# Order and queues of the first loads in a fused LoRA and gated feed-forward kernel

## The chip, the cores and the metric

The kernel runs on one core of one Trainium2 chip. The metric is the device time of one execution, in microseconds. The kernel before took 476.14 us (median of three runs, 475.85 to 476.36).

## The reference

The input x has 8 sequences of 256 tokens with 1024 features. Each sequence picks one of 8 adapters of rank 16; the adapted tokens pass a gated feed-forward layer whose operands are rounded to 8-bit floats, and x is added again:

```python
B_sel = B[adapter_ids]; A_sel = A[adapter_ids]
Bx  = einsum('bni,bri->bnr', x, B_sel)
h   = einsum('bnr,bor->bno', Bx, A_sel)
gate = fake_quant_fp8(h) @ gate_w.T * gate_w_scale      # 2752 x 1024
up   = fake_quant_fp8(h) @ up_w.T * up_w_scale          # 2752 x 1024
hidden = silu(gate) * up
out  = x + fake_quant_fp8(hidden) @ down_w.T * down_w_scale   # 1024 x 2752
```

The weights come as float32 values that are already rounded to 8 bits.

## The kernel before

The 2048 tokens are cut into four blocks of 512 (t = 0 to 3), the features into eight rows of 128 (k), the inner dimension into 22 chunks (c; the last one is half as wide). Activations lie transposed, features on partitions and tokens along the free dimension. Block t of x is `xs[t]`, 128 x 8 x 512 float32, 2 MB.

For each block TensorE first computes `bx` = B x (`two_times_b`, 64 small matmuls for blocks 0 and 1, each of which contracts 128 features of 128 tokens with one adapter's B). Two copies bring the result into SBUF as `bm`, and `two_times_a` multiplies it by A (64 small matmuls into `c`), which VectorE and ScalarE scale and round to 8 bits as `xg[t]`. Then `gate_up(c, t)` computes sixteen matmuls of 128 x 512 into two accumulators `y`, eight for the gate and eight for the up half. ScalarE applies the SiLU and VectorE the product, which is `hid[c]`. One weight tile `w_gu` of 1 MB holds both halves of a chunk; five buffers hold them. The first five chunks run for block 0, then for block 1, then for blocks 2 and 3 together; the other chunks run for all four blocks each. At last the down projection (`yd`) runs over eight output rows, and VectorE adds x. ScalarE also sums the low bits of the weights and the squares of the activations beside all this, as guards for a general path that is not taken here.

TensorE's instructions are kept in program order. The opening of that order is: sixteen matmuls on zeros (`warm`), `bx` of block 0 with four more filler matmuls after row k = 3, seven fillers, the `c` matmuls, `gate_up(0, 0)` in the order "two rows of gate, two of up", then the next chunks:

```python
pass_time(warm, 16, TB)
bm = two_times_b(0, lambda k: pass_time(warm, 4) if k == 3 else None)
pass_time(warm, 7)
two_times_a(0, bm)
gate_up(0, 0, turns=(2, 2, 2, 2))
```

Row k of `bx` needs the B of both sequences of the block and row k of x; `c` needs all of A for the block. The first half of tile w0 serves the first eight y matmuls of `gate_up(0, 0)`, its second half the last eight; `gate_up(1, 0)` needs w1.

The loads are issued on the queues of the engines. `adapter_of` (line 363) loads an adapter's number into a register of the issuing engine, which must wait for the transfer of `ids`; `load_b` (line 366) and `load_a_two` (line 373) use it as an address. `load_x` is line 381, `load_gate_up` line 391. Almost everything goes through SyncE's queue, in program order; ScalarE issues `ids` and one B. DMA issues share eight completion semaphores in turn, so an issue can wait for the landing of the one eight places ahead. The array `x4` holds x in pieces of `PIECES[t]` rows each, each piece contiguous; block 0 is cut 4, 3, 1.

A DMA of the down projection's tail weights (`wt`, line 656) stands late in the program but is issued after block 3's loads, ahead of weight tile 5.

Of the kernel before, what the change touches and what calls it, by code (L numbers as in the profile page):

```python
# [25 lines left out]
NH = H // P  # L26
# [9 lines left out]

KS = NH // 2

PIECES = ((4, 3, 1), (4, 3, 1), (NH,), (NH,))
FP8_MAX = 448.0  # L40

SAME_MAX = 240.0
# [17 lines left out]
def x_of(x4, t, k):  # L60

    first = 0
    for n in PIECES[t]:
        if k < first + n:
            break
        first += n
    at = (t * NH + first) * P * TB
    piece = x4[at : at + n * P * TB].rearrange("(p k n) -> p k n", p=P, k=n)
    return piece, first
# [214 lines left out]
def adaln_ffn(  # L284
# [13 lines left out]
    nc = tc.nc  # L298
# [31 lines left out]
    wt = kept.tile([P, NH, P], F32, name="w_dt")  # L330
# [6 lines left out]
    with ExitStack() as fast:  # L337
# [5 lines left out]
        xs = [acts.tile([P, NH, TB], F32, name=f"x{t}") for t in range(NTB)]  # L343
# [8 lines left out]
        b_two = [lora.tile([P, 2 * BROW + R], F32, name=f"b{t}") for t in range(2)]  # L352
# [9 lines left out]
        def adapter_of(batch, queue):  # L362
            return queue.value_load(ids_i[0:1, batch : batch + 1], min_val=0, max_val=7)  # L363

        def load_b(b, i, adapter, queue):
            queue.dma_start(  # L366
                out=b[:, i * BROW : (i + 1) * BROW], in_=b8[bass.ds(adapter * P, P), :]
            )

        def load_a_two(t, j, adapter):  # L370
            for g in range(2):
                row = 32 * (2 * g + j) + R * j
                nc.sync.dma_start(
                    out=a_two[t][row : row + R],
                    in_=a8[bass.ds(adapter * 2 * R + g * R, R), :],
                )

        def load_x(t, k):
            piece, first = x_of(x4, t, k)
            ks = slice(first, first + piece.shape[1])  # L380
            nc.sync.dma_start(out=xs[t][:, ks, :], in_=piece)

        w_of = {}

        def load_gate_up(c, parts=1):
            n = NH if c == NI - 1 else 2 * NH
            w = wpool.tile([P, 2 * NH, P], F32, tag="w", name="w_gu")[:, :n]
            src = gate_up_of(w_gu, c).rearrange("p (k n) -> p k n", n=P)
            n //= parts
            for i in range(parts):  # L390
                nc.sync.dma_start(out=w[:, bass.ts(i, n)], in_=src[:, bass.ts(i, n)])
            w_of[c] = w

        load_x(0, 0)
        load_b(b_two[0], 0, adapter_of(0, nc.scalar), nc.scalar)
        second = adapter_of(1, nc.sync)
        load_b(b_two[0], 1, second, nc.sync)


        load_x(0, 4)  # L400
        load_a_two(0, 1, second)
        load_a_two(0, 0, adapter_of(0, nc.sync))
        load_x(0, 7)
        for c in range(NFIRST):
            load_gate_up(c, parts=1 if c else 2)
        adapters = [adapter_of(2 + q, nc.sync) for q in range(6)]
# [4 lines left out]
        for j in range(2):  # L411
            load_a_two(1, j, adapters.pop(0))

        for t in (2, 3):
            load_x(t, 0)
            for q in (2 * t - 4, 2 * t - 3):
                load_b(b_four, q, adapters[q], nc.sync)
        for q in range(4):
            nc.sync.dma_start(
                out=a_four[32 * q : 32 * q + R], in_=aT[bass.ds(adapters[q] * R, R), :]  # L420
# [48 lines left out]
        def multiply(*args, **kwargs):  # L469
            tc.keep_in_program_order(nc.tensor.matmul(*args, **kwargs))  # L470

        def pass_time(to, n, size=P):

            for i in range(n):
                multiply(
                    to[:, :size],
                    lhsT=zeros[:, :P],
                    rhs=zeros[:, :size],
                    start=(i == 0),
                    stop=(i == n - 1),  # L480
                )

        def times_b(bx, b, n, quads, between=None):


            for k in range(NH):
                for q, (i, row, t, cols) in enumerate(quads):
                    at = i * BROW + k * R - row
                    multiply(
                        bx[q][32 * q : 32 * (q + 1)],  # L490
                        lhsT=b[:, at : at + 32],
                        rhs=xs[t][:, k, cols],
                        start=(k == 0),
                        stop=(k == NH - 1),
                    )
                if between:
                    between(k)

        def two_times_b(t, between=None):


            n = SEQ // 2
            quads = [
                (j, R * j, t, slice(at, at + n))
                for half in range(2)
                for j in range(2)
                for at in (j * SEQ + half * n,)
            ]
            bx = [psum.tile([P, n], F32, tag="ps", name=f"bx{half}") for half in range(2)]
            times_b([bx[q // 2] for q in range(4)], b_two[t], n, quads, between)  # L510
            bm = lora.tile([P, 2, n], F32, tag="bm2", name="bm2", bufs=2)
            for other in range(2):
                for half, copy in enumerate((nc.vector.tensor_copy, nc.scalar.copy)):
                    to = half ^ other
                    tc.keep_in_program_order(
                        copy(  # L516
                            bm[64 * to : 64 * (to + 1), other],
                            bx[half][64 * half : 64 * (half + 1)],
                        )
                    )  # L520
            return bm
# [110 lines left out]

        warm = psum.tile([P, TB], F32, tag="ps", name="warm")
        pass_time(warm, 16, TB)
        bm = two_times_b(0, lambda k: pass_time(warm, 4) if k == 3 else None)
        pass_time(warm, 7)
        two_times_a(0, bm)
        gate_up(0, 0, turns=(2, 2, 2, 2))
# [14 lines left out]
        for c in range(NFIRST, NI):  # L653
            load_gate_up(c)
            if c == NI - 2:
                nc.sync.dma_start(out=wt, in_=w_d_tail)
            for t in range(NTB):
                gate_up(c, t)

# [70 lines left out]
        for k in range(NH - 1):  # L730
# [23 lines left out]
            first = k % 2 == 0  # L754
# [29 lines left out]
    with found_others.Else():  # L784

        k = NH - 1
# [9 lines left out]
        t, cols = NTB - 1, slice(cut, TB)  # L796
# [88 lines left out]
```

## Time and profile before

| | us |
|---|---|
| median of three runs | 476.14 |
| the profiled execution, whole time | 477.12 |
| its span, first to last instruction | 475.3 |
| TensorE busy | 469.8 |
| ScalarE busy | 192.5 |
| VectorE busy | 105.6 |
| GpSimd busy | 1.0 |

The page gives the busy time of each engine and the share of the span. The chain follows the work that ended last backwards, at each step to what released it. A timeline lists instructions in order of time, equal neighbours merged, with the idle time before them and what ended it in brackets; "SPq" is SyncE's queue issuing a DMA, and its length is that of the issue, not of the transfer. Of 53.44 MB that the DMA engines moved, most belong to later stages; over the first 17.21 us they moved 320 GB/s on average, afterwards 105 GB/s. The granted TensorE clock is full throughout.

Landings of the first transfers (issue plus time to landing): x rows 0 to 3 at 5.8 us, B at 6.1 and 6.2, x rows 4 to 6 at 8.3, x row 7 at 9.6, w0's first half at 10.9, w1 at 17.2.

### The profile page before, as it was taken

How to read it: one execution, taken by the hardware profiler on the slowest of the kernel's cores; microseconds unless marked ns; L12 is line 12 of the kernel's file. 1: busy time of each engine (PE TensorE's matmuls, PEld its weight loads, DVE VectorE, ACT ScalarE, POOL GpSimd, SP SyncE). 2: the span in 40 equal slices, each digit the busy share in tenths (PEclk: the TensorE clock that was granted, in tenths of full speed). 3: DMA queues.
4: the chain of work that ended last, by engine and by line, in shares of the span. 5: the costliest groups of instructions: out<-in, count | busy, mean ns of one | idle time of the engine just before them, and what ended most of it. 6: DMA issues, size and time to landing. Idle time of an engine off the chain costs nothing.

```text
span 475.3 us, 6009 instructions
## 1 busy us (share of the span) xinstructions
PE 469.8 (99%) x2514; PEld 217.0 (46%) x2514; DVE 105.6 (22%) x163; ACT 192.5 (40%) x249; POOL 1.0 (0%) x7
## 2 busy tenths in 40 slices
PE   8999999999999999999999999999999999999997
PEld 4454544444444444444444444444444444444444
DVE  1333432121212222121212212132120121031031
ACT  1322447995556654533454554359212022021000
POOL 0000000000000000000000000000000000000000
PEclk9999999999999999999999999999999999999999
DMA  8995013422222112222211111123335255063031
GB/s 291 406 405 186 1 48 133 176 88 90 88 88 89 24 66 89 90 88 88 90 30 60 44 62 56 61 83 123 103 146 161 64 185 161 22 213 114 3 116 66
DMA packets 13780, 53.44 MB, mean 112 GB/s; under 512 B 1650, under 2 KB 2930, under 8 KB 10674
## 3 DMA queue, kind: packets, MB, share of 16 engines
q1 hardware_dynamic: 13600, 52.92, 32.1%
q8 instruction: 21, 0.34, 0.3%
q14 instruction: 13, 0.11, 0.1%
q10 hardware_dynamic: 146, 0.07, 0.0%
HBM read 44.60 MB, written 8.39 MB: 111 GB/s over the span
## 4 chain that ended last, share of the span: by engine, by line
PE 96%; DMA 3%; SPq 0%; issue 0%; DVE 0%
PE y L470 62%; PE yd L470 31%; DMA w_gu<-w_gu 2%; PE c L470 1%; PE bx L470 1%; DMA x<-x 1%; DMA ids_i<-ids 0%; SPq L363 0%; SPq L366 0%; DVE o L695 0%; PE count L470 0%
## 5 line engine op out<-in xcount | busy, mean ns | idle before, releaser
L470 PE MATMUL y<-xg,w_gu 128*128 128x512 fp8e4 x1376 | 298.4, 379 | 0.9 <-DMA w_gu<-w_gu 0.9
L470 PEld LDWEIGHTS <-w_gu 128*128 128x128 bf16 x1376 | 134.0, 98 | 163.8 <-DMA w_gu<-w_gu 1.8
L470 PE MATMUL yd<-hid,w_d 128*128 128x512 fp8e4 (+2 forms) x693 | 146.0, 373 | 0.0
L609 ACT ACTIVATE g<-y,gate_s 128x512 f32<-128x512 f32 (+1 forms) x88 | 59.8, 681 | 137.2 <-PE y L470 137.2
L610 DVE SCALAR_TENSOR_TENSOR hid<-y,up_by_down,g 128x512 fp8e4<-128x512 f32 x84 | 63.1, 751 | 220.3 <-PE y L470 162.2
L470 PEld LDWEIGHTS <-w_d 128*128 128x128 bf16 x693 | 66.6, 98 | 79.0 <-issue 1.7
L456 ACT ACTIVATE junk<-w_d 128x1408 bf16<-128x1408 uint16 (+1 forms) x16 | 21.2, 1324 | 88.4 <-DMA w_d<-w_d 88.3
L695 DVE SCALAR_TENSOR_TENSOR o<-yd,down_s,x 128x512 f32<-128x512 f32 x28 | 20.0, 748 | 107.4 <-PE yd L470 92.8
L456 ACT ACTIVATE junk<-w_gu 128x2048 bf16<-128x2048 uint16 (+1 forms) x22 | 41.0, 1863 | 0.0
L463 ACT ACTIVATE junk<-hid 128x2048 bf16<-128x2048 fp8e4 x21 | 40.0, 1905 | 0.4
L463 ACT ACTIVATE junk<-xg 128x2048 bf16<-128x2048 fp8e4 x8 | 15.3, 1909 | 0.3
L528 ACT ACTIVATE xg<-c,inv 128x512 fp8e4<-128x512 f32 x16 | 9.7, 688 | 8.6 <-PE c L470 8.6
L526 DVE TENSOR_SCALAR xg<-c,inv 128x512 fp8e4<-128x512 f32 x16 | 10.9, 744 | 2.8 <-PE c L470 2.8
L470 PE MATMUL warm<-zeros 128*128 128x512 bf16 (+1 forms) x27 | 6.5, 402 | 1.2 <-DVE zeros L309 1.2
L695 DVE SCALAR_TENSOR_TENSOR o<-yd,down_s,xg 128x512 f32<-128x512 f32 (+2 forms) x5 | 3.2, 644 | 12.3 <-PE yd L470 12.3
L516 ACT COPY bm<-bx 64x128 f32<-64x128 f32 x4 | 1.0, 262 | 9.7 <-PE bx L470 9.6
L470 PE MATMUL bx<-x,b 128*32 128x128 f32 x128 | 4.3, 276 | 0.6 <-DMA x<-x 0.6
L470 PEld LDWEIGHTS <-zeros 128*128 128x128 bf16 x27 | 2.6, 116 | 4.7 <-issue 3.0
L470 PE MATMUL c<-bm,a 32*128 32x128 f32 x128 | 4.3, 277 | 0.0
L456 ACT ACTIVATION_READ_ACCUMULATOR junk<-w_gu 128x1 f32 x22 | 4.2, 191 | 0.0
L470 PEld LDWEIGHTS c<-bm,a 32*128 32x128 f32 x128 | 3.9, 186 | 0.5 <-ACT bm L516 0.4
L470 PE MATMUL yd<-hid_tail,w_dt 64*128 64x512 bf16 (+1 forms) x32 | 4.1, 377 | 0.0
(47 smaller groups left out, 41.0 us busy)
## 6 DMA issues: line engine op xcount, KB each, us to landing
w_gu<-w_gu SPq DMA_DIRECT2D x20, 1024.0 KB, 4.8
outT<-o SPq DMA_DIRECT2D x31, 256.0 KB, 2.2
w_d<-w_d SPq DMA_DIRECT2D x8, 704.0 KB, 4.8
w_d<-w_d SPq DMA_DIRECT2D x8, 640.0 KB, 3.9
x<-x SPq DMA_DIRECT2D x2, 2048.0 KB, 11.1
x<-x SPq DMA_DIRECT2D x2, 1024.0 KB, 8.6
x<-x SPq DMA_DIRECT2D x2, 768.0 KB, 9.5
w_gu<-w_gu SPq DMA_DIRECT2D x3, 512.0 KB, 3.8
```

The source lines that it names most:

```text
L456: nc.scalar.activation(junk_like(w), low(w), AF.Copy, accum_out=lows[:rows, column : column + 1])
L463: nc.scalar.activation(junk_like(q), q, AF.Square, accum_out=squares[:rows, column : column + 1])
L470: tc.keep_in_program_order(nc.tensor.matmul(*args, **kwargs))
L516: copy(bm[64 * to : 64 * (to + 1), other], bx[half][64 * half : 64 * (half + 1)],)
L526: nc.vector.tensor_scalar(to, c, scale, None, ALU.mult, saturate=False)
L528: nc.scalar.activation(to, c, AF.Copy, scale=scale, saturate=False)
L609: nc.scalar.activation(g[rows], gates, AF.Silu, scale=gate_s[: gates.shape[0]])
L610: nc.vector.scalar_tensor_tensor(to, in0=ups, scalar=up_by_down[rows], in1=g[rows], op0=ALU.mult, op1=ALU.mult, saturate=False,)
L695: nc.vector.scalar_tensor_tensor(o, in0=y, scalar=down_s, in1=x, op0=ALU.mult, op1=ALU.add)
```

## The change

Block 0 of x is cut into pieces of 2, 2, 3 and 1 rows. They are the first four issues on SyncE's queue, and the first five weight tiles follow at once. Both loads of B for block 0 go on ScalarE's queue, the four loads of A on GpSimd's, each with its own register load. The four filler matmuls move from behind row 3 to behind row 6. Later on, x of blocks 2 and 3 and the tail weights are each loaded in two halves instead of one transfer. The amount of data and all other arithmetic stay.

```diff
-PIECES = ((4, 3, 1), (4, 3, 1), (NH,), (NH,))
+PIECES = ((2, 2, 3, 1), (4, 3, 1), (NH,), (NH,))
...
-        def load_a_two(t, j, adapter):
+        def load_a_two(t, j, adapter, queue=nc.sync):
             for g in range(2):
                 row = 32 * (2 * g + j) + R * j
-                nc.sync.dma_start(
+                queue.dma_start(
...
-        def load_x(t, k):
+        def load_x(t, k, n=NH):
             piece, first = x_of(x4, t, k)
-            ks = slice(first, first + piece.shape[1])
-            nc.sync.dma_start(out=xs[t][:, ks, :], in_=piece)
+            n = min(n, piece.shape[1])
+            nc.sync.dma_start(out=xs[t][:, k : k + n, :], in_=piece[:, k - first : k - first + n])
...
-        load_x(0, 0)
-        load_b(b_two[0], 0, adapter_of(0, nc.scalar), nc.scalar)
-        second = adapter_of(1, nc.sync)
-        load_b(b_two[0], 1, second, nc.sync)
-
-
-        load_x(0, 4)
-        load_a_two(0, 1, second)
-        load_a_two(0, 0, adapter_of(0, nc.sync))
-        load_x(0, 7)
+
+
+        for k in (0, 2, 4, 7):
+            load_x(0, k)
+        for j in range(2):
+            load_b(b_two[0], j, adapter_of(j, nc.scalar), nc.scalar)
+            load_a_two(0, j, adapter_of(j, nc.gpsimd), nc.gpsimd)
         for c in range(NFIRST):
             load_gate_up(c, parts=1 if c else 2)
...
         for t in (2, 3):
-            load_x(t, 0)
+            for k in (0, KS):
+                load_x(t, k, KS)
...
-        bm = two_times_b(0, lambda k: pass_time(warm, 4) if k == 3 else None)
+        bm = two_times_b(0, lambda k: pass_time(warm, 4) if k == 6 else None)
...
-                nc.sync.dma_start(out=wt, in_=w_d_tail)
+                for ks in (slice(0, KS), slice(KS, NH)):
+                    nc.sync.dma_start(out=wt[:, ks], in_=w_d_tail[:, ks])
```

## Prediction

> **What bounds the kernel now.** I read the page's busy table, then the chain that ended last, then TensorE's and SyncE's instructions over the first microseconds.
>
> ```profile
> span 475.3 us, 6009 instructions
> PE 469.8 (99%) x2514; PEld 217.0 (46%) x2514; DVE 105.6 (22%) x163; ACT 192.5 (40%) x249; POOL 1.0 (0%) x7
> ```
>
> TensorE is idle for 475.3 - 469.8 = 5.5 us. Of this, 2.8 us is the tail after 472.50 and 1.2 us precedes the first warm-up matmul; what waits for data is all in the opening. The chain in order of time says where it hands over to TensorE for good:
>
> ```profile
> 3.33 4.97 DMA x<-x
> ...
> 8.32 8.85 DMA w_gu<-w_gu
> 17.17 0.05 issue
> 17.21 13.12 PE y L470 x60
> ```
>
> The last two columns ahead of the name are start and length. From 17.21 us on everything is TensorE, back to back. What sets that point is the landing of the second weight tile, w1. TensorE's timeline:
>
> ```profile
> 1.20 5.58 PE L470 MATMUL warm<-zeros 128*128 128x512 bf16 x16 [1.20 <-DVE zeros L309]
> 6.71 1.08 PE L470 MATMUL bx<-x,b 128*32 128x128 f32 x32
> ...
> 8.34 0.86 PE L470 MATMUL bx<-x,b 128*32 128x128 f32 x24 [0.22 <-DMA x<-x]
> 9.59 0.43 PE L470 MATMUL bx<-x,b 128*32 128x128 f32 x8 [0.38 <-DMA x<-x]
> ...
> 10.45 2.17 PE L470 MATMUL c<-bm,a 32*128 32x128 f32 x64
> 12.58 1.89 PE L470 MATMUL y<-xg,w_gu 128*128 128x512 fp8e4 x8
> 14.70 1.90 PE L470 MATMUL y<-xg,w_gu 128*128 128x512 fp8e4 x8 [0.23 <-DMA w_gu<-w_gu]
> 17.21 2.98 PE L470 MATMUL y<-xg,w_gu 128*128 128x512 fp8e4 x13 [0.62 <-DMA w_gu<-w_gu]
> ```
>
> Two waits for x, two for weights. At the steady pace (13.12 us / 60 = 219 ns) sixteen y matmuls need 3.5 us; here 17.21 - 12.58 = 4.63 us, so the weights cost 1.13 us. SyncE's queue shows why data are late:
>
> ```profile
> 0.75 0.38 SPq L381 DMA_DIRECT2D x<-x  x1
> 2.92 0.37 SPq L366 DMA_DIRECT2D b<-b  x1
> 3.33 0.45 SPq L381 DMA_DIRECT2D x<-x  x1
> 4.00 2.58 SPq L373 DMA_DIRECT2D a<-a  x4
> 6.62 0.42 SPq L381 DMA_DIRECT2D x<-x  x1
> 7.09 2.99 SPq L391 DMA_DIRECT2D w_gu<-w_gu  x6
> ```
>
> B, A and the register loads stand between the x pieces, so the weights are not asked for before 7.09 us. The one-microsecond windows show what that costs: 418, 404, 406 and 412 GB/s from 3 to 7 us, then
>
> ```profile
> 7.00:8.00 1.00, 1.00 (x36) 0.75 (x24) 0.00 (x0) 0.00 (x0) 0.00 (x0) 1.00 0.92 275
> 8.00:9.00 1.00, 0.78 (x27) 0.59 (x24) 0.00 (x0) 0.00 (x0) 0.00 (x0) 1.00 0.85 293
> ```
>
> The last column is GB/s.
>
> **What the Trainium skill says.** "DMA: Bandwidth & Descriptors", section "SWDGE vs HWDGE vs iDMA": a DMA from GpSimd gets its descriptors from software on that engine, one from SyncE or ScalarE from hardware. The kernel before issues none from GpSimd, so no trace shows its price here. The same page, "Issuing engines are not separate DMA queues": all issuers share the same 16 engines, and more issuers save only issue time. That fits: the stream runs near 410 GB/s from one queue. "TensorE: Matmul & The Clock Gate", Part 1: a cold TensorE runs at half rate, and about 3.4 us of idling makes it cold. In the trace the warm-up's weight loads are 0.43 us apart until about 5.3 us, then twice as dense; no later gap reaches 1 us.
>
> **The change part by part.**
>
> *SyncE's queue.* Removed from it ahead of the weights: one B, four A and two register loads. Ahead of them stay four x pieces at about 0.42 us each, so the issues start at 0.75, 1.17, 1.6 and 2.05 us and the first half of w0 at 2.5 us instead of 7.09. Behind it w0's second half waits for the landing of ids (1.93 us now), and w1 to w4 wait for the four x pieces, because completion semaphores are reused; more than 1 MB is outstanding at each such point, so the DMA engines don't run dry.
>
> *x.* The pieces hold 2.10 MB, with B (0.14) and A (0.13) 2.37 MB. By 3.0 us 0.21 MB had moved (66 and 147 GB/s in two windows). At 410 GB/s the rest takes 5.3 us, 8.3 us in all; before, a piece landed some 0.8 us after its bytes were through by this sum (the second piece: 7.45 against 8.30). So the last x lands near 9.1 us, instead of 9.57 (6.62 plus 2.9 to landing). I allow 8.8 to 9.5.
>
> *B.* ScalarE issues its first at 2.88 us as now. The second comes after another register load and address step (0.27 + 0.15 + about 0.3 us) at about 4.05 us and lands 3.2 us later (what the first took): 7.25 us instead of 6.2. Now the bx matmuls start at 6.71, when warm-up ends; this moves them to 7.25. Without waits the 64 take 1.9 us (as 30.34 to 32.22 us for the next block), the four filler matmuls 0.25: 9.4 us. The last x at 9.1 is hidden behind them, so the bound is about even. bx ends near 9.5 instead of 9.9, and c can start near 10.1 instead of 10.45.
>
> *A on GpSimd.* Its memset ends at 1.55 us; the ids land at 1.93, the register is ready near 2.85. Lower end: issues as short as SyncE's 0.33 us and a landing in 4.1 us (today's median): 2.85 + 4 x 0.33 + 0.55 for the second register + 4.1 = 8.8 us. Upper end: the price on "DMA: Bandwidth & Descriptors", "Anatomy of one DMA — SWDGE (gpsimd) path", is 2.0 us fixed plus bytes at 436 GB/s, 2.08 us for 32 KB; four of them end to end give 2.85 + 8.3 + 0.55 = 11.7 us, more if the loaded engines delay them. I take 1 us of GpSimd each, as an estimate between these: the last is issued at 6.4 us and lands at 8.5 to 10.5. Nothing else queues on GpSimd but a branch at the end; behind A stand only the c matmuls. A is thus just hidden behind bx.
>
> *Where the stall goes.* c at 10.1 gives y at 12.23 (2.13 later, as 10.45 to 12.58) and the second y group at 15.75, if w1 is there. So w1 remains the last to arrive. Its start is set by bytes: now it lands at 17.17, and the windows from 7 to 17 us fall short of 410 GB/s by 0.52 MB, or 1.25 us. The change fills the holes that come from late issue but not those of small rows: B's 544 byte rows, the 2 KB rows of A and of the last x piece are still there. I take two thirds, 0.84 us: w1 at 16.35 us. The bounds are 0.3 and 1.3 us (zero if all holes are small rows; more than 1.3 would need a faster first 3 us).
>
> *Later edits.* Halving x of blocks 2 and 3 and the down tail adds three issues of about 0.4 us on SyncE, before a wait for a weight buffer that lasts 30.3 us (42.5 to 67.5): hidden. Block 1's x is issued after w0 has landed and moves with the stream: its last piece lands at 30.5 now (17.2 + 13.3) and is needed near 31.8. With both 0.8 us earlier the slack stays 1.3 us. If that cover failed, the cost would be microsecond for microsecond.
>
> *Sum.* 17.21 to 16.37 us: -0.84 us. All 455 us behind shift as they are: profiled span 475.3 to 474.5, this execution's 477.12 to 476.3. The median of the runs is 0.98 lower than that execution; the difference carries over: 476.14 - 0.84 = 475.3.
>
> **The rivals.** *Fully packed stream.* If w1 lands by 15.75 to 16.2, the gain is 1.0 to 1.45 us: 474.7 to 475.1. For it: two thirds of the holes stand exactly where issues were late. Against it: the engines show 0.85 to 0.92 busy inside them, so they were not empty.
>
> *A late on GpSimd (the slower side).* It decides from the point where the last A lands after 17.21 - 3.5 - 2.13 = 11.6 us. At 2.6 us each the last lands at 2.85 + 10.4 + 0.55 = 13.8: +2.2 us, 478.3; at 3 us each 15.4: +3.8 us, 479.9. For it: four dependent-looking small transfers on one software path into a full stream; ready time is 1 us short of what the upper price gives. Against it: 5 us of room if issues overlap.
>
> *B's second half late.* It decides at 17.21 - 3.5 - 2.13 - 0.7 - 2.15 = 8.7 us, against 7.25; at 10 us it would be +1.3 us, 477.4.
>
> *Hidden anyway.* If w1 comes as late as now because all SDMA bytes before it are the same, the time stays 475.9 to 476.1.
>
> **How the numbers follow.** A measurement of this kernel can tell about 0.2%, 0.95 us, from no change. Main case with "hidden anyway", 475.2 to 476.4: 0.40. Packed stream, 474.7 to 475.2: 0.28. A late, 477.1 to 480: 0.25. B late, 477.1 to 478: 0.07. So faster 0.28, same 0.40, slower 0.32. The range leaves out about 0.1 above and 0.07 below: 474.8 to 478.6; the likeliest case's own is 475.2 to 476.4.
>
> **What the profile after would show.** Right: weight issues from 2.5 us, no x wait over 0.2 us, c near 10.1 us, a y start after w1 near 16.4, DMA above 380 GB/s from 3 to 12 us. Wrong: c waiting for DMA a beyond 11.6 us, bx waiting for b beyond 8.7, or GpSimd issues well over 1 us each. A gap of more than 3.4 us would also cost clock: sixteen matmuls at half rate, 3.5 us more.

## The result, and the profile after

The changed kernel took 481.96 us (median of four runs, 480.86 to 482.47), the kernel before 476.25 (four runs, one more than above): a ratio of 1.0114, interval 1.0090 to 1.0138. The change costs 5.7 us, where a gain of 0.8 us was forecast.

The page of the changed kernel:

```profile
span 480.0 us, 6020 instructions
PE 470.7 (98%) x2514; PEld 218.3 (45%) x2514; DVE 105.5 (22%) x163; ACT 192.6 (40%) x249; POOL 3.1 (1%) x11
```

The span of the profiled execution grew by 4.7 us, TensorE's busy time by 0.9 us. Idle time is 9.3 us instead of 5.5. The chain that ended last in order of time (start, length, what) names the new hand-over:

```profile
4.17 7.65 DMA b<-b
11.82 0.04 issue
11.86 3.14 PE bx L468 x54
...
16.18 2.11 PE c L468 x63
18.29 16.52 PE y L468 x76
```

Before, the chain ran through x and the weights. Now it runs through the second B: 7.65 us from issue at 4.17 to landing at 11.82. TensorE's timeline of the changed kernel:

```profile
1.33 5.21 PE L468 MATMUL warm<-zeros 128*128 128x512 bf16 x16 [1.33 <-DVE zeros L309]
9.97 0.38 PE L468 MATMUL bx<-x,b 128*32 128x128 f32 x2 [3.43 <-DMA b<-b]
11.86 3.14 PE L468 MATMUL bx<-x,b 128*32 128x128 f32 x54 [1.51 <-DMA b<-b]
...
16.11 2.18 PE L468 MATMUL c<-bm,a 32*128 32x128 f32 x64
18.25 5.12 PE L468 MATMUL y<-xg,w_gu 128*128 128x512 fp8e4 x23
```

The waits for x and for weights are gone; y runs without a break from 18.25. In their place stand two waits for B. The first two bx matmuls use the first sequence's B and start at 9.97; the next need the other B and start at 11.86, instead of 6.71.

The one-microsecond windows show a second effect; the third number from the end is the granted clock of TensorE, the last is GB/s:

```profile
5.00:6.00 1.00, 1.00 (x7) 0.45 (x5) 0.00 (x0) 0.00 (x0) 0.48 (x1) 1.00 0.82 281
...
11.00:12.00 1.00, 0.14 (x4) 0.14 (x8) 0.00 (x0) 0.00 (x0) 0.00 (x0) 0.70 1.09 388
12.00:13.00 1.00, 1.00 (x24) 0.92 (x25) 0.00 (x0) 0.00 (x0) 0.00 (x0) 0.50 1.03 422
...
14.00:15.00 1.00, 1.00 (x21) 0.65 (x12) 0.00 (x0) 0.00 (x0) 0.00 (x0) 0.60 1.09 451
```

After the long idle stretch TensorE ran at half its clock: the windows' 0.70, 0.50 and 0.60 put this from about 11.4 to 14.8 us, 3.4 us long. The column can't be read so for the warm-up: it shows 1.00 there too, in both kernels, while the weight loads come only every 0.43 us (until 5.3 us before, until 4.6 here) and then twice as dense. So "full throughout", as said above of the kernel before, holds only from about 5 us on. And with everything queued early the DMA engines still fell to 281 GB/s near 5 us.

The sum closes. The second y group would start at 18.25 + 3.5 = 21.75 us, against 17.21 before: +4.54 of the span's 4.7. Of these, +5.15 are the later bx start (11.86 - 6.71); from bx's start to c's the kernel before took 3.74 us and this one 4.25, +0.51, although the waits for x are gone, since the clock is low (the 54 bx matmuls take 3.14 us; at full clock they take 1.73, as a longer warm-up will show); -1.13 are the weights' waits that fell away. This sum is of the two profiled executions. The medians lie further apart, 5.7 us, because the profiled execution of the kernel before was 0.9 us above its median and this one 0.4 below.

### The profile page after: what moved, and what is told of

Same layout as the page of the kernel before. It is cut to its first block, busy times and chain, and to the rows that moved or that the text cites. A ratio compares the mean times of both kernels' runs of the same rounds, so it can differ in the third digit from the quotient of the medians.

```text
span 480.0 us, 6020 instructions
## 1 busy us (share of the span) xinstructions
PE 470.7 (98%) x2514; PEld 218.3 (45%) x2514; DVE 105.5 (22%) x163; ACT 192.6 (40%) x249; POOL 3.1 (1%) x11
## 4 chain that ended last, share of the span: by engine, by line
PE 97%; DMA 2%; ACTq 0%; ACT 0%; issue 0%; DVE 0%
PE y L468 62%; PE yd L468 31%; PE bx L468 2%; PE c L468 2%; DMA b<-b 2%; ACT L307 0%; PE warm L468 0%; ACTq L363 0%; ACTq L366 0%; ACTq L306 0%; DVE o L694 0%; PE count L468 0%
## 5 line engine op out<-in xcount | busy, mean ns | idle before, releaser
L524 DVE TENSOR_SCALAR xg<-c,inv 128x512 fp8e4<-128x512 f32 x16 | 10.9, 742 | 2.8 <-PE c L468 2.8
L468 PE MATMUL bx<-x,b 128*32 128x128 f32 x128 | 5.9, 335 | 4.9 <-DMA b<-b 4.9
L468 PEld LDWEIGHTS bx<-x,b 128*32 128x32 f32 x128 | 4.5, 136 | 6.4 <-issue 3.9
L694 DVE SCALAR_TENSOR_TENSOR o<-yd,down_s,xg 128x512 f32<-128x512 f32 (+2 forms) x5 | 3.2, 643 | 12.3 <-PE yd L468 12.3
```

Source lines behind the costliest of these rows:

```text
L524: nc.vector.tensor_scalar(to, c, scale, None, ALU.mult, saturate=False)
L694: nc.vector.scalar_tensor_tensor(o, in0=y, scalar=down_s, in1=x, op0=ALU.mult, op1=ALU.add)
```

## The experiments

Two theories were set against each other. **Full stream**: a small transfer, on whatever queue, lands only after what was issued before it on SyncE's queue has gone through; B and A are late because x and weights were put ahead of them. **Slow path**: ScalarE's second load and GpSimd's loads are slow in themselves. Beside them: what the low clock costs, and whether the smaller edits matter.

**Weights asked for later (w_later).** B and A keep their queues; only what is queued beside them changes.

```diff
+        adapters = [adapter_of(2 + q, nc.sync) for q in range(6)]
         for c in range(NFIRST):
             load_gate_up(c, parts=1 if c else 2)
-        adapters = [adapter_of(2 + q, nc.sync) for q in range(6)]
```

> The changed kernel, with the six register loads of later adapters moved ahead of the weight tiles on SyncE, so that the weights are asked for about 3.5 us later (near 6.2 us instead of 2.7). Theory 'full stream' (a small transfer on any queue lands only when what was issued before it on SyncE's queue has passed): at B's two issues only the 2.1 MB of x stand ahead, so both B land near 8.5 to 9 us instead of 9.9 and 11.9, bx starts near 8.8 with the clock still full, c near 11.6, and the time is 476 to 477. Rival 'slow path' (ScalarE's second load and GpSimd's loads are slow whatever stands beside them): B lands at 9.9 and 11.9 as before the edit, and the time stays near 482.

TensorE's timeline of this kernel:

```profile
8.65 0.38 PE L468 MATMUL bx<-x,b 128*32 128x128 f32 x2 [2.17 <-DMA b<-b]
9.55 1.73 PE L468 MATMUL bx<-x,b 128*32 128x128 f32 x54 [0.53 <-DMA b<-b]
```

B landed at 8.5 and 9.5 us, near what "full stream" had (5.5 and 5.4 us from issue instead of 6.8 and 7.7), with unchanged issue times on an unchanged queue. So in these executions the weights beside it cost B 1.3 and 2.3 us, and "slow path" falls for ScalarE. The time was only partly as expected: the profiled execution took 477.93 us, but the median is 480.24 (477.93 to 481.38), 1.0069 times before (1.0048 to 1.0091). The clock divides the eight runs: two with a mean granted clock of 0.999 took 477.9 and 478.3 us, six with 0.995 or 0.996 took 480.0 to 481.4.

**Both B on ScalarE in the kernel before (before_b_scalar).**

```diff
-        second = adapter_of(1, nc.sync)
-        load_b(b_two[0], 1, second, nc.sync)
+        load_b(b_two[0], 1, adapter_of(1, nc.scalar), nc.scalar)
+        second = adapter_of(1, nc.sync)
```

> The kernel before, with both B of block 0 on ScalarE's queue, all else as it was. 'Full stream': the second B is issued near 4.1 us behind 1.8 MB of x and lands near 8.3 us, bx starts 1.6 us later than before, but the weights come a little earlier and take up most of it: 475.8 to 476.6. 'Slow path': the second B lands near 11.8 us as in the changed kernel, c near 16, 480 to 481.

TensorE's timeline of this kernel:

```profile
8.40 0.38 PE L470 MATMUL bx<-x,b 128*32 128x128 f32 x2 [2.11 <-DMA b<-b]
8.93 1.07 PE L470 MATMUL bx<-x,b 128*32 128x128 f32 x30 [0.16 <-DMA b<-b]
```

The second B landed at 8.9, not 11.8. But also the first B, on the same queue as before, came at 8.3 instead of 6.1: with one issue fewer on SyncE the second x piece was being issued from about 3.2 us, just ahead of the first B at 3.26 (2.88 before; the ids came 0.4 us later in this execution). The forecast of the time missed: 478.25 us, 1.0041 (1.0024 to 1.0058). The weights were asked for later, not earlier (from 8.28 us, when the first B had landed), but they were not missed: w1 landed at 16.6 us, and in the trace y runs without a break from 13.91. That puts the second y group at 17.4, 0.2 us later than before, and the profiled execution, 477.27 us, is the fastest of the twelve. Three of the others, with a mean granted clock of 0.993 to 0.996, took 479.8 to 481.4 us; the other eight, up to 478.8, have no trace.

**A on GpSimd in the kernel before (before_a_gpsimd).** `load_a_two` takes a queue, as in the change.

```diff
...
-        load_a_two(0, 1, second)
-        load_a_two(0, 0, adapter_of(0, nc.sync))
+        load_a_two(0, 1, adapter_of(1, nc.gpsimd), nc.gpsimd)
+        load_a_two(0, 0, adapter_of(0, nc.gpsimd), nc.gpsimd)
```

> The kernel before, with the four A of block 0 on GpSimd's queue, all else as it was; the last x and the weights then follow at once on SyncE. Both theories that hold for B give A about 6 us from issue to landing in a full stream: the last A lands near 12 us, c starts there, and the time is 476.5 to 477.0, since w1 is early. If A in fact comes in time (by 10.2 us), w1 sets the end and the time is 475.0 to 475.5.

TensorE's timeline of this kernel:

```profile
11.84 2.50 PE L470 MATMUL c<-bm,a 32*128 32x128 f32 x64 [1.38 <-DMA a<-a]
14.27 12.05 PE L470 MATMUL y<-xg,w_gu 128*128 128x512 fp8e4 x55
```

c waits for A; the last of the four, issued at about 6.2 us, took 6.0 us to land, and c had already begun on the others. The time is 477.89 us, 1.0023 (1.0015 to 1.0032): A's move alone costs 1.1 us, a little more than expected. The weights were ready (no wait ahead of y), so their early issue, at 4.54 us instead of 7.09, bought nothing.

**A longer warm-up in the changed kernel (warm_longer).**

```diff
-        pass_time(warm, 16, TB)
+        pass_time(warm, 38, TB)
```

> The changed kernel with 38 instead of 16 matmuls on zeros at the start, which keep TensorE busy until about 11.7 us, when the second B has landed. If the cold clock between 11 and 15 us is a part of the loss, bx takes 1.6 us less and the time falls to about 480.4; if the clock costs nothing beside the wait for B, it stays near 482.

TensorE's timeline of this kernel:

```profile
1.33 10.11 PE L468 MATMUL warm<-zeros 128*128 128x512 bf16 x38 [1.33 <-DVE zeros L309]
...
12.49 1.73 PE L468 MATMUL bx<-x,b 128*32 128x128 f32 x54 [0.71 <-DMA b<-b]
```

The same 54 matmuls took 1.73 us instead of 3.14, and all four runs have a mean granted clock of 1.000, where the changed kernel's have 0.993 to 0.995. The time is 480.82 us, 1.1 us below the changed kernel (the intervals of the two ratios overlap; the 1.4 us in the traces are the firmer figure): a fifth to a quarter of the loss is the clock. B landed 0.6 us later in this execution, 8.3 us from issue, although the loads are those of the changed kernel: landings of the same program differ by that much between executions.

**Order and queues put back, the rest kept (order_undone).** In place of the diff's new load block stand x rows 0 to 3 in two pieces, B on ScalarE and SyncE, x, four A on SyncE, the last x.

```diff
-        for k in (0, 2, 4, 7):
-            load_x(0, k)
-        for j in range(2):
-            load_b(b_two[0], j, adapter_of(j, nc.scalar), nc.scalar)
-            load_a_two(0, j, adapter_of(j, nc.gpsimd), nc.gpsimd)
+        load_x(0, 0)
+        load_x(0, 2)
+        load_b(b_two[0], 0, adapter_of(0, nc.scalar), nc.scalar)
+        second = adapter_of(1, nc.sync)
+        load_b(b_two[0], 1, second, nc.sync)
+        load_x(0, 4)
+        load_a_two(0, 1, second)
+        load_a_two(0, 0, adapter_of(0, nc.sync))
+        load_x(0, 7)
```

> The changed kernel with only the order and the queues of block 0's first loads put back (first x rows, B on ScalarE and SyncE, next x, four A on SyncE, last x, weights); the smaller x pieces, the filler after row 6 and the later halved transfers stay. If the queue order is the whole cause, B lands near 6.2 us, w1 near 17.2, and the time is that of the kernel before within 0.2%. If the later halved transfers or the filler carry part of the loss, it stays over 0.2% slower.

477.06 us, 1.0009 (0.9999 to 1.0018) of before. Pieces, filler and later halved transfers cost nothing that can be measured; the order and the queues are the cause.

**B moved forward (b_sync_early).** The other loads follow it later.

```diff
-        for k in (0, 2, 4, 7):
-            load_x(0, k)
+        load_x(0, 0)
         for j in range(2):
-            load_b(b_two[0], j, adapter_of(j, nc.scalar), nc.scalar)
+            load_b(b_two[0], j, adapter_of(j, nc.sync), nc.sync)
             load_a_two(0, j, adapter_of(j, nc.gpsimd), nc.gpsimd)
+        for k in (2, 4, 7):
+            load_x(0, k)
```

The second x piece needs no register and goes out ahead of B, so 1 MB stands in front of it.

> The changed kernel with both B on SyncE, ahead of the last two x pieces; A stays on GpSimd. 'Full stream': both B have 1 MB of x ahead of them and land at 6.2 to 6.9 us, bx starts near 6.9. Then A is next: issued up to 6.1 us beside a full stream it lands near 12 us and holds c back to there, so y runs 0.4 to 0.8 us later than before: 0.1 to 0.2% slower than before. If only B was the trouble and A is in time, c starts near 10.4 and the kernel is 0.15 to 0.3% faster than before.

TensorE's timeline of this kernel:

```profile
7.06 1.07 PE L469 MATMUL bx<-x,b 128*32 128x128 f32 x30 [0.23 <-DMA b<-b]
9.69 0.86 PE L469 MATMUL bx<-x,b 128*32 128x128 f32 x24 [1.56 <-DMA x<-x]
...
11.67 2.17 PE L469 MATMUL c<-bm,a 32*128 32x128 f32 x64
```

477.19 us, 1.0013 (1.0004 to 1.0022): with B in front, nearly the whole loss is gone. The size was as expected, the reason not: c was held back by the third x piece, issued only after both B, and not by A. The last A landed at 11.6, just before c began at 11.67, so A was the next bound all the same.

**A longer warm-up with the later weights (w_later_warm).** w_later's edit, and 29 matmuls instead of 16.

> The kernel with the weights asked for later (w_later), and 29 instead of 16 matmuls on zeros, so that TensorE is busy until about 9.4 us. Its unprolonged form spread from 477.9 to 481.4 us. If the spread and the median come from a clock that falls in some executions during the wait for B, the times gather near 477.5 to 478; if they come from the transfers, the spread stays.

Its four runs lie between 478.93 and 479.40 us, 1.0046 (1.0029 to 1.0063); those of w_later spread over 3.4 us. With the longer warm-up all four have a mean granted clock of 1.000, and w_later's runs fall into two groups by their clock (above): the spread goes with the clock, and a TensorE kept busy removes it. The median missed by a microsecond: in the profiled execution the register load that needs the ids began at 3.0 us instead of 2.1, and both B were issued that much later. Why the ids came later is open.

**A on ScalarE in the kernel before (a_on_scalar).** With A off SyncE's queue but still ahead of the weights (`load_a_two` takes a queue here too):

```diff
...
-        load_b(b_two[0], 0, adapter_of(0, nc.scalar), nc.scalar)
-        second = adapter_of(1, nc.sync)
-        load_b(b_two[0], 1, second, nc.sync)
+        first = adapter_of(0, nc.scalar)
+        load_b(b_two[0], 0, first, nc.scalar)
+        load_b(b_two[0], 1, adapter_of(1, nc.sync), nc.sync)
         load_x(0, 4)
-        load_a_two(0, 1, second)
-        load_a_two(0, 0, adapter_of(0, nc.sync))
         load_x(0, 7)
+        load_a_two(0, 1, adapter_of(1, nc.scalar), nc.scalar)
+        load_a_two(0, 0, first, nc.scalar)
```

> The kernel before with the four A on ScalarE's queue behind the first B; SyncE issues first x, B, second x, last x and then the weights. The A are issued by 5.7 us with about 1.3 MB ahead of them, so by 'full stream' they land near 9 to 9.5 us, ahead of c at 10.4; the weights start near 6.2 instead of 7.1 us, w1 lands 0.5 to 0.9 us earlier: 0.1 to 0.2% faster than before. If ScalarE's queue is slow by itself, A lands after 11.6 us and it is slower.

TensorE's timeline of this kernel:

```profile
8.40 1.41 PE L469 MATMUL bx<-x,b 128*32 128x128 f32 x32 [0.77 <-DMA x<-x]
...
10.24 2.17 PE L469 MATMUL c<-bm,a 32*128 32x128 f32 x64
12.37 13.97 PE L469 MATMUL y<-xg,w_gu 128*128 128x512 fp8e4 x64
```

476.13 us, 0.9984 (0.9977 to 0.9992): faster than the kernel before by 0.16%. The weights' wait is gone (w1 lands at 14.8 us), c starts 0.2 us earlier, A is in time.

**B on SyncE behind all of x (b_sync_behind_x).** The changed kernel with `nc.sync` in both `load_b` calls, which stand behind the four x pieces and ahead of the weights.

> The changed kernel with both B on SyncE, behind the four x pieces and ahead of the weights, A on GpSimd as it was. If what counts is what stands ahead and not the queue, B, issued near 3 and 3.8 us behind 2.1 MB of x, lands near 8.5 and 9.2 us, as B on ScalarE's queue did when the weights came later (8.5 and 9.6), and the time is near that kernel's, 477.5 to 480, well below the changed kernel's 482. If ScalarE's queue itself cost time, B lands 2 us or more earlier than 8.5.

TensorE's timeline of this kernel:

```profile
10.29 3.36 PE L468 MATMUL bx<-x,b 128*32 128x128 f32 x56 [2.79 <-DMA b<-b]
```

One of its one-microsecond windows:

```profile
12.00:13.00 1.00, 1.00 (x27) 1.00 (x23) 0.00 (x0) 0.00 (x0) 0.00 (x0) 0.50 1.03 426
```

B took 6.4 and 5.7 us from issue to landing (5.5 and 5.4 on ScalarE's queue in w_later, behind the same x): SyncE's queue is no faster. The time, 480.65 us, 1.0090 (1.0072 to 1.0108), is above what was expected, for two reasons. The issue came late, at 3.73 us: SyncE's register load began at 2.7 us, when its four x issues were done (GpSimd's began at 2.1). And the clock fell: it was at half from 9.9 to 13.3 us, the 56 matmuls took 3.36 us, and all four runs have a mean granted clock of 0.993 to 0.996.

**The small transfers side by side.** "Ahead" is what had been issued before, less what the windows show as moved by then, in MB; times are in us:

```
kernel            transfer          queue    issued   ahead     to landing
b_sync_early      second B          SyncE    4.21     0.36      2.8
b_sync_early      first B           SyncE    3.05     0.72      2.8
before            first B           ScalarE  2.88     0.86      3.2
before_b_scalar   second B          ScalarE  4.40     1.15      4.5
before_b_scalar   first B           ScalarE  3.26     1.47      5.0
w_later           second B          ScalarE  4.15     1.47      5.4
w_later           first B           ScalarE  3.01     1.82      5.5
changed           first B           ScalarE  3.02     2.28      6.8
changed           second B          ScalarE  4.17     2.46      7.7
warm_longer       first B           ScalarE  3.01     2.31      7.0
warm_longer       second B          ScalarE  4.14     2.48      8.3
w_later_warm      second B          ScalarE  5.12     1.08      5.2
w_later_warm      first B           ScalarE  3.98     1.34      6.0
b_sync_behind_x   second B          SyncE    4.88     1.15      5.7
b_sync_behind_x   first B           SyncE    3.73     1.51      6.4
b_sync_early      first A           GpSimd   3.63     0.57      2.4
w_later           last A            GpSimd   6.11     0.78      3.7
w_later           first A           GpSimd   3.65     1.63      5.3
changed           first A           GpSimd   3.66     2.62      6.2
changed           last A            GpSimd   6.11     4.13      6.2
```

Broadly, the more stands ahead, the longer a transfer takes to land, on each of the three queues. "1 us plus the bytes ahead at 400 GB/s" comes within 0.8 us for the seven B from "before, first" to "changed, second" (0.86 MB gives 3.2 us, 2.28 MB gives 6.7); for the other eight it is up to 1.8 us too short, so the bytes ahead are not the whole account. GpSimd's A levels off: behind 2.6 and 4.1 MB it took 6.2 us alike.

Nor does a small transfer wait until all that was issued before it has gone through, as "full stream" says. In the changed kernel the last x piece, the first half of w0 and the first B were issued in this order, at 2.25, 2.72 and 3.02 us (the last column is us to landing):

```profile
x<-x SPq DMA_DIRECT2D x1, 256.0 KB, 7.9
w_gu<-w_gu SPq DMA_DIRECT2D x1, 512.0 KB, 9.5
b<-b ACTq DMA_DIRECT2D x1, 68.0 KB, 6.8
```

B landed first, at 9.8 us, before x at 10.15 and w0 at 12.2. The packets say more. The first number is that of the packets of a queue in one microsecond, q1 is SyncE's queue and q10 ScalarE's; from 5 to 6 us, and from 7 to 8:

```profile
q1 hardware_dynamic: 53, 0.28, 81.6%
...
q1 hardware_dynamic: 118, 0.34, 87.5%
q10 hardware_dynamic: 74, 0.04, 12.1%
```

No packet of B moved before 6.9 us, 3.9 us after the first issue; from then on they ran between SyncE's, and the last one moved at 11.1. In w_later they ran from 6.5 to 8.6 us, in the kernel before from 5.0 to 5.7. So putting the weights beside B hardly moved its first packet (0.4 us), but stretched the two B from 2.1 to 4.2 us. What holds the first packet back for 2.1 us (before) to 3.9 us, and why A levels off, no run shows.

## Why the prediction was wrong

**What bounds the kernel** was read rightly: only the opening waits for data, and all behind it shifted as it was (264.29 us of y, 121.08 and 28.41 of yd in both chains).

**The step that failed is B's.** It took the second B's landing as issue plus 3.2 us, "what the first took". That 3.2 us was measured behind 0.86 MB. The change puts 2.1 MB of x and then weights ahead, and B took 6.8 and 7.7 us. The prediction had the point from which it decides (8.7 us) and the rival (a chance of 0.07, 477.1 to 478 us), but no reason for B to be late; B landed at 11.8, so its own rule gives 3.1 us more, and the low clock adds 1.4: together the 4.5 us by which the second y group came later. A landing time was carried over as if it belonged to the operation, when it belonged to the load around it. The early x and weights, costed for their gain alone, are what made B late.

**A's step** used 1 us of GpSimd for each and a landing at 8.5 to 10.5. GpSimd was busy 0.48 to 0.62 us for each, less than estimated, but the transfer took 6.1 to 6.4 us and the last landed at 12.3. In the changed kernel B hides it; alone it costs 1.1 us (before_a_gpsimd). The rival "A late" had the right threshold, 11.6 us, and the wrong reason: not issues of 2.6 us each on GpSimd, but a late landing, which fell to 2.4 us where only 0.57 MB stood ahead.

**The weights' step** came out, and better than forecast. It supposed that two thirds of the missing bytes came from late issue (the two windows that it shows hold half of them, 0.25 of 0.53 MB) and put w1 at 16.35 us. The weights were asked for 4.4 us earlier, and w1 landed at 15.8 us (issued at 4.17, 11.6 us to landing) instead of 17.2, although w0's first half came later, at 12.2 instead of 10.9. None of it counted, since y began only at 18.25 and the second y group needed w1 at 21.75. What failed here is the claim that w1 remains the last to arrive: it was B. Nor did the rate rise above 380 GB/s from 3 to 12 us; it was 348, before 363. What makes the engines fall to 281 GB/s near 5 us with 3 MB queued is open.

**The last x** was put at 9.1 us (8.8 to 9.5) and landed at 10.15.

**The clock** was named only at the end, as the cost of a gap of over 3.4 us. The Trainium skill, "TensorE: Matmul & The Clock Gate", Part 1, puts the cold state after an idle window of about 3.4 us. The changed kernel agrees: one wait of 3.4 us and one of 1.5 close behind it took the clock to half for 3.4 us, and bx's 54 matmuls cost 1.4 us more. But b_sync_behind_x does not: there one wait of 2.8 us was enough, and the measurement decides. Nor is there one fixed length: a wait of 2.2 us left the clock full in the traced run of w_later, whose other runs had a lower mean clock in six cases of seven.

**The skill on queues.** "Issuing engines are not separate DMA queues" was cited for the bandwidth alone; that transfers from all issuers interleave is the other half of it, and a queue of its own did not make B arrive sooner: 5.5 and 5.4 us on ScalarE's queue in w_later, 2.8 us on SyncE's in b_sync_early. "Queues, rings and completion order" on the same page says the engines take turns between queues packet by packet. From 6.9 us on the trace agrees (118 packets of SyncE's queue and 74 of ScalarE's from 7 to 8 us), and B did pass the last x piece; but for 3.9 us after its issue it had no turn, and that the section does not tell.

**The later edits** were rightly costed at nothing (order_undone).

## What to carry to other kernels

A landing time read from a trace holds for the load that was queued around that transfer; when large transfers are moved ahead of it or beside it, price every small transfer anew, on its own queue or not. Issue the small operand that gates the first matmul before the big stream, and let the stream start behind it: in b_sync_early this took back nearly the whole loss. A wait of TensorE can cost more than its length: here a wait of 2.8 us, and one of 3.4 with one of 1.5 behind it, each brought 3.4 us at half clock.

## What was not expected of the hardware

Transfers of 32 KB on GpSimd's queue took between 2.4 and 6.4 us to land in b_sync_early and the changed kernel, with the same 0.48 to 0.62 us on GpSimd for each. A transfer of 68 KB on a queue of its own had no packet moved for 2.1 to 3.9 us after its issue while another queue was loaded. And the DMA rate of the opening varies by itself: from 3 to 12 us the changed kernel had 348 GB/s and warm_longer, with the same loads, 363; w_later had 387 and w_later_warm, with the same loads and later ids, 356. So that asking earlier for more data lowers the rate is not shown, and neither is it for the 391 GB/s of a_on_scalar, where the weights were held back to 6 us.
